# Attention steps of three, three and two key tiles in a two-layer graph network kernel

## The chip, the core and the metric

The kernel runs on one core of a Trainium2 chip. The core has a matrix engine (TensorE, "PE" in the profile; its weight loads are "PEld"), VectorE ("DVE"), ScalarE ("ACT"), GpSimd ("POOL") and SyncE ("SP", which here only issues DMAs). Each works through its own queue in order and waits for the others on semaphores. TensorE writes into PSUM, eight banks of 128 partitions by 512 fp32 numbers; VectorE and ScalarE read it from there. The metric is the device time of one execution in microseconds (us).

## The reference

Sixteen graphs of 1024 nodes with 256 features share one adjacency matrix. Layer 0 is an attention whose queries come through a graph product; layer 1 is a normalised graph convolution with two dense layers and two batch norms.

```python
# layer 0, on h = relu(layernorm(x)); fea = transpose(h)
c_adj = mean(fea, axis=1)
diff = c_adj[:, None, :] - c_adj[:, :, None]
A = abs(abs(sigmoid(diff) - 0.5) - 0.5) * 2.0
A_s = (A + transpose(A)) * 0.5
g = relu(einsum('bcn,bnm->bcm', fea, adj * A_s) * para)     # queries
k, v = split(h @ kv_w)                                      # 4 heads of 64
attn = softmax(q @ k^T * scale);  x = x + attn @ v
# layer 1, on h = relu(layernorm(x))
agg = einsum('nm,bmd->bnd', A_hat, h)                       # A_hat: normalised adj + eye
h1 = relu(batchnorm(agg @ W1.T + b1))
x = x + batchnorm(h1 @ W2.T + b2)
```

Everything is fp32.

## The kernel before

**Attention.** A unit is one graph, one pair of heads `k` (two heads of 64 rows) and one half `f` of the queries (512 columns): 16 x 2 x 2 = 64 units. The keys are eight tiles of 128. A step (`scores`, L1071) takes two key tiles: for each of them four 64x64 matmuls (two heads `e`, two halves `c` of the tile) write two PSUM banks (L1081), one per head, and one exponential of 128x1024 (L1089) turns both into a tile `p` in SBUF. The pool `ps_sc` holds two such score tiles, four banks; `ps_o` holds one bank for the output `o`, and `ps_mm` three for everything else: all eight. In the trace every matmul shows as two records (fp32 goes through the array twice), so a key tile has eight score records.

`Unit.add` (L1104) adds the `p` tiles into `acc` on VectorE, for the softmax's denominators. `Unit.values` (L1115) multiplies the `p` tiles of the step before with the values (L1124): a step on TensorE is scores of step s, then values of step s - 1, then background. At a unit's end `fold` sums `acc` on VectorE, `sums` sends two small matmuls (L1173) through TensorE, `finish`/`gather` and `add_output` put the result into `xs`.

**Order.** It is written out by hand: `attention` (L1240) runs over the steps and between them draws pieces of work from a generator, `background(b)` (L964), until their costs reach the amount `due` at this step. For graph `b` the background computes keys, values and queries of graph `b + 1` (`keys_values` L672, `queries` L537), layer 1's graph product and first dense layer of graph `b - 1` (`aggregate`, `hidden`), and the norm of graph `b + 2` (`summed` L943). The engines' queues get the instructions in exactly this order.

**Weights.** `weigh(b)` (L477) makes `adj * A_s` in eight blocks: per block two ScalarE `Abs` (L508), one `Tanh` (L516), one VectorE multiplication with an adjacency block (L495). `weave(main, (i, side))` draws one slot of `side` with each piece of `main` from the i-th on; `double` draws two slots at once.

**Squares.** `squares(b)` (L432) transposes the normed features in 32x32 squares on VectorE and writes them to DRAM through GpSimd's queue; `gathered` (L446) reads them back, transposed, as `ht`, through SP's queue. The buffers with the tag `para` (two of 128x512) hold the factor of the queries (`load_para`, multiplied in at L557) and temporaries of layer 1.

**A second version of both layers** (`shifted_attention`) follows under a branch that is taken only if the softmax without a shift overflowed; in these runs it isn't taken.

After attention, `second` computes the second dense layer and the output from about 2130 us on; the change doesn't touch it.

Of the kernel before, what the change touches and what calls it, by code (L numbers as in the profile page):

```python
# [10 lines left out]
F32 = mybir.dt.float32  # L11
# [6 lines left out]
P = 128  # L18
# [5 lines left out]
def gnn_two_layers_kernel(  # L24
# [74 lines left out]
    def layers(shifted):  # L99
# [14 lines left out]

        p4 = attn.enter_context(tc.tile_pool(name=f"p4_{kind}", bufs=4, side="right"))
        ps_sc = attn.enter_context(
            tc.tile_pool(name=f"ps_sc_{kind}", bufs=2, space=PSUM, side="right")
        )
# [83 lines left out]
        nc.sync.dma_start(out=kvw, in_=kv_w.rearrange("(k p) j -> p k j", p=P))  # L202
        rows = big.tile([P, NH, NT], F32, name="rows")

# [23 lines left out]

        deg_sm = big.tile([P, 6, NT], F32, name="deg")
        later = {}  # L230
        row, diag, col, deg, tmp_deg, dinv = (deg_sm[:, i, :] for i in range(6))

# [199 lines left out]
        def squares(b):  # L432

            for k in range(CC):
                sq = p1.tile([P, N], F32, tag="sq", name=f"sq_{b}_{k}")
                nc.vector.transpose(
                    sq.rearrange("p (i t s) -> p i t s", i=NS, s=SQ),
                    hs["a", b][:, :, k * P : (k + 1) * P].rearrange("p t (i s) -> p i t s", s=SQ),  # L440
                )
                nc.gpsimd.dma_start(out=hsq_d[b][:, k], in_=sq)
                for _ in range(3):
                    yield 0.0
# [32 lines left out]
        def weigh(b):  # L477
# [11 lines left out]
            for slot in range(2 * NH * NP + 1):  # L489
# [27 lines left out]
                yield 0.0  # L517

        AHEAD = 6
        IDLE = 28  # L520
# [443 lines left out]
        def background(b):  # L964

            if b == 0:
# [59 lines left out]
        def shifted_attention(b):  # L1026
            for hd in range(HEADS):
                k, e = divmod(hd, 2)
                r = slice(e * HD, (e + 1) * HD)
                for t in range(NT):  # L1030
                    name = f"{b}_{hd}_{t}"
                    sc = ps_sc.tile([P, N], F32, tag="sc", name=f"sc_{name}")
                    for g in range(NH):
                        nc.tensor.matmul(
                            sc[:, g * FB : (g + 1) * FB],
                            qs[b][k][r, t * P : (t + 1) * P],
                            ks[b][k][r, g * FB : (g + 1) * FB],
                            start=True,
                            stop=True,
                        )  # L1040
                    sm = p2.tile([P, 3], F32, tag="smx", name=f"smx_{name}")
                    nc.vector.tensor_reduce(sm[:, 0:1], sc, AX.X, ALU.max, negate=True)
                    pr = p4.tile([P, N], F32, tag="p", name=f"p_{name}")
                    nc.scalar.activation(
                        pr, sc, AF.Exp, bias=sm[:, 0:1], accum_out=sm[:, 1:2]
                    )
                    nc.vector.reciprocal(sm[:, 2:3], sm[:, 1:2])
                    pt = p4.tile([P, N], F32, tag="p", name=f"pt_{name}")
                    for g in range(NH):
# [21 lines left out]
        def scores(b, k, f, g):  # L1071


            made = []
            for m in (2 * g, 2 * g + 1):
                sc = ps_sc.tile([P, 2, FB], F32, tag="sc", name=f"sc_{b}_{k}_{f}_{m}")
                for e in range(2):
                    r = slice(e * HD, (e + 1) * HD)
                    for c in range(2):
                        part = slice(c * HW, (c + 1) * HW)  # L1080
                        nc.tensor.matmul(  # L1081
                            sc[part, e, :],
                            ks[b][k][r, m * P + c * HW : m * P + (c + 1) * HW],
# [3 lines left out]
                        )  # L1087
                pr = p4.tile([P, 2, FB], F32, tag="p", name=f"p_{b}_{k}_{f}_{m}")
                nc.scalar.activation(pr, sc, AF.Exp)  # L1089
                made.append(pr)  # L1090
            return made

        class Unit:
# [21 lines left out]
            def values(self, g, prs):  # L1115

                b, k, f = self.at
                if g == 0:
                    self.o = ps_o.tile([P, FB], F32, tag="o", name=f"o_{self.name}")
                for i, pr in enumerate(prs):  # L1120
                    m = 2 * g + i
                    for e in range(2):
# [7 lines left out]
                        )  # L1130
                if g == NG - 1:
                    self.os = p2.tile([P, FB], F32, tag="os", name=f"os_{self.name}")
# [107 lines left out]
        def attention():  # L1240

            units = [Unit(b, k, f) for b in range(B) for k in range(CC) for f in range(NH)]
            steps = [(u, g) for u in units for g in range(NG)]
            per_graph = CC * NH * NG
# [3 lines left out]
            for s in range(len(steps) + 2):  # L1248
                if s < len(steps):
# [10 lines left out]
                    made = scores(*unit.at, g)  # L1260
                    due = total * (s % per_graph + 1) / per_graph
                    if b == B - 1:
                        due -= 0.5 * min(s % per_graph + 1, (per_graph - 1 - s % per_graph) * 0.75)
                else:
# [13 lines left out]
                if before is not None:  # L1278
                    (last, g_last), prs = before
                    last.values(g_last, prs)  # L1280
                    if g_last == NG - 1:
# [431 lines left out]
```

## Time and profile before

| | |
|---|---|
| median of 3 runs | 2460.07 us (2460.07 to 2460.52) |
| profiled execution, timed | 2460.34 us |
| its span, first to last instruction | 2458.6 us |
| TensorE's clock granted | 0.993 of full speed |
| ScalarE waits for scores (L1089) | 649.5 us |
| VectorE busy | 2003.9 us |
| DMA, mean over the span | 178 GB/s |
| first and last score matmul | 54.1 and 2124.1 us |

In a timeline a row is a run of like instructions: start and length in us, engine, line, operation, tiles ("written<-read"), shapes, how many, and in brackets the idle time of the engine just before with what ended it. In the table of groups "x512 | 495.4, 1020 | 649.5 <-PE" reads: 512 instructions, 495.4 us busy, 1020 ns each on average, 649.5 us of idle time of that engine before them, ended by PE. Matmul records overlap, since the array is pipelined: a record of 0.59 us is followed by the next one after about 0.43.

### The profile page before, as it was taken

To read this page: it belongs to the slowest core of one execution; us is meant where nothing else is said; L and a number is where in the kernel's file an instruction comes from. 1 tells how busy PE (TensorE), PEld (TensorE's weight loads), DVE (VectorE), ACT (ScalarE), POOL (GpSimd) and SP (SyncE) were. 2 spreads that over 40 slices of the span, in tenths; PEclk is the share of its full clock that TensorE was granted. 3 is DMA by queue.
4 is the path that set the end of the run, shared out by engine and by line. 5 is a ranking of instruction groups with operands and counts; after the bars stand their busy time and mean duration, and the time that the engine had idled before them with its cause. 6 is when DMAs were issued, how large, how long until landed. Compare 5 with 4: busy or idle time off the path is not lost. (4 is left out here: it accounts for less than half of the span.)

```text
span 2458.6 us, 35932 instructions
## 1 busy us (share of the span) xinstructions
PE 2412.4 (98%) x13290; PEld 832.6 (34%) x13290; DVE 2003.9 (82%) x3103; ACT 1257.7 (51%) x1870; POOL 559.5 (23%) x645
## 2 busy tenths in 40 slices
PE   9999999999999999999999999999999999999994
PEld 4333333333333333333333333333333332334444
DVE  5678888988888888888898888888888878767775
ACT  7874554545464545445454546454454534335554
POOL 1381202111111212020211212121202103136652
PEclk9999999999999999999999999999999999999997
DMA  4675545363645554453536355544545353456559
GB/s 146 204 242 182 172 138 179 118 229 125 209 139 193 171 189 163 158 171 126 209 117 231 120 201 160 197 164 167 172 134 188 116 201 142 152 197 230 196 193 372
DMA packets 204553, 437.18 MB, mean 178 GB/s; under 512 B 21456, under 2 KB 96720, under 8 KB 200272
## 3 DMA queue, kind: packets, MB, share of 16 engines
q1 hardware_dynamic: 173328, 327.29, 39.7%
q0 software_dynamic: 31040, 107.50, 11.6%
q8 instruction: 107, 1.75, 0.3%
q14 instruction: 78, 0.64, 0.1%
HBM read 331.36 MB, written 103.35 MB: 177 GB/s over the span
## 5 line engine op out<-in xcount | busy, mean ns | idle before, releaser
L1089 ACT ACTIVATE p<-sc 128x1024 f32<-128x1024 f32 x512 | 495.4, 1020 | 649.5 <-PE sc L1081 649.5
L1113 DVE TENSOR_TENSOR acc<-acc,p 128x1024 f32<-128x1024 f32 x384 | 469.8, 1223 | 58.2 <-ACT p L1089 36.9
L1081 PE MATMUL sc<-q,k 64*64 64x512 f32 x4096 | 498.6, 602 | 0.5 <-ACT p L1089 0.5
L1124 PE MATMUL o<-p,v 128*64 128x512 f32 x2048 | 494.7, 604 | 0.0
L174 PE MATMUL pa<-aht,h_b 128*64 128x512 f32 x1536 | 346.0, 592 | 1.1 <-ACT h_b L368 1.1
L174 PE MATMUL pg<-w,x_h 128*64 128x512 f32 x1472 | 332.0, 592 | 0.0
L1081 PEld LDWEIGHTS sc<-q,k 64*64 64x64 f32 x4096 | 131.5, 132 | 336.4 <-issue 287.8
L1124 PEld LDWEIGHTS o<-p,v 128*64 128x64 f32 x2048 | 124.6, 136 | 297.7 <-issue 251.2
L1142 POOL DMA_DIRECT2D out_d<-os x58 | 32.9, 568 | 803.2 <-DVE os L1138 803.2
L495 DVE SCALAR_TENSOR_TENSOR w<-w,adj 128x1024 f32<-128x1024 f32 x128 | 164.9, 1288 | 46.1 <-ACT w L516 45.1
L174 PEld LDWEIGHTS pa<-aht,h_b 128*64 128x64 f32 x1536 | 110.1, 137 | 220.6 <-issue 207.8
L174 PEld LDWEIGHTS pg<-w,x_h 128*64 128x64 f32 x1472 | 105.7, 137 | 210.1 <-issue 198.4
L508 ACT ACTIVATE w<-cbc,csum 128x512 f32<-128x512 f32 x256 | 170.3, 716 | 0.0
L516 ACT ACTIVATE w<-w 128x1024 f32<-128x1024 f32 x128 | 135.6, 1059 | 2.5
L571 DVE TENSOR_TENSOR w<-w,w 128x1024 f32<-128x1024 f32 x112 | 134.6, 1232 | 1.5
L174 PE MATMUL pv<-kvw_f,ht 128*64 128x256 f32 x1024 | 116.1, 379 | 0.0
L174 PE MATMUL pk<-ht,kvw_f 128*64 128x512 f32 x512 | 115.2, 593 | 0.2 <-ACT ht L430 0.2
L174 PE MATMUL py<-at,w 128*64 128x512 f32 x464 | 112.6, 593 | 0.8 <-DVE at L729 0.7
L174 PE MATMUL py<-at,w1s 128*64 128x512 f32 x448 | 107.9, 595 | 0.0
L1453 ACT ACTIVATE yin_f<-yin_f,sm_f 128x512 f32<-128x512 f32 x128 | 93.5, 803 | 19.0 <-DMA yin_f<-y_d 17.0
L826 POOL DMA_DIRECT2D y_d<-y x112 | 61.6, 550 | 145.1 <-DVE y L846 75.8
L1160 DVE TENSOR_REDUCE part<-acc 128x16 f32<-128x512 f32 x128 | 87.8, 686 | 4.4
(197 smaller groups left out, 2968.6 us busy)
## 6 DMA issues: line engine op xcount, KB each, us to landing
aht<-aht_d SPq DMA_DIRECT2D x224, 512.0 KB
adj<-in_adj_dram SPq DMA_DIRECT2D x128, 512.0 KB
y_d<-y POOLq DMA_DIRECT2D x128, 256.0 KB, 3.0
yin_f<-y_d SPq DMA_DIRECT2D x32, 1024.0 KB
para<-in_para_dram SPq DMA_DIRECT2D x64, 256.0 KB
x_d<-x_x POOLq DMA_DIRECT2D x16, 1024.0 KB, 5.1
xo_f<-x_d SPq DMA_DIRECT2D x32, 512.0 KB
out_dram<-xo_f POOLq DMA_DIRECT2D x32, 512.0 KB, 11.1
```

The lines of the kernel that those rows point to most:

```text
L174: nc.tensor.matmul(dst[r], left[:, r], right, start=start, stop=stop)
L495: nc.vector.scalar_tensor_tensor(w, w, 1.0, a, op0=ALU.add, op1=ALU.mult)
L508: nc.scalar.activation(w[:, t, :].rearrange("p (t q) -> p t q", q=P), cbc[:, q * NT // NH : (q + 1) * NT // NH], AF.Abs, bias=csum[:, th * ...
L516: nc.scalar.activation(made[i], made[i], AF.Tanh, scale=-0.5 / C)
L571: nc.vector.tensor_sub(block(i)[part], block(x)[part], block(y)[part])
L826: nc.gpsimd.dma_start(out=y1_d[i][:, j, :], in_=y)
L1081: nc.tensor.matmul(sc[part, e, :], ks[b][k][r, m * P + c * HW : m * P + (c + 1) * HW], qs[b][k][r, f * FB : (f + 1) * FB], start=True, sto ...
L1089: nc.scalar.activation(pr, sc, AF.Exp)
L1113: nc.vector.tensor_add(self.acc, self.acc, pr)
L1124: nc.tensor.matmul(self.o[r, :], vs[b][k][:, m, r], pr[:, e, :], start=(m == 0), stop=(m == NT - 1),)
L1160: nc.vector.tensor_reduce(self.part[:, e, :], acc.rearrange("p (c s) -> p c s", s=SQ), AX.X, ALU.add)
L1453: nc.scalar.activation(y, y, AF.Relu, bias=sh[:, j : j + 1], scale=scale[:, j : j + 1])
```

## The change

A unit now has three steps, with key tiles (0,1,2), (3,4,5) and (6,7). A score tile is one PSUM bank, for one head, out of four; each has an exponential of its own (128x512). The `p` tiles get a pool of their own, `p6`, with five buffers (before: four). The schedule's amounts are restated by key tiles instead of steps. The small `sums` matmuls come at the end of a step instead of its middle.

`squares` works on half of the nodes at a time, in buffers of the tag `para` instead of one of their own, and its first half is woven into the norm. Row sums of the adjacency (`rows`, `deg`) move into a part of `stats1` that isn't yet in use. In the first graph the weights' first slots are drawn singly; in the others two slots are drawn ahead of the keys, and doubling starts one piece later. `shifted_attention` is adapted to the smaller score tiles.

```diff
+        p6 = attn.enter_context(tc.tile_pool(name=f"p6_{kind}", bufs=5, side="right"))
         ps_sc = attn.enter_context(
-            tc.tile_pool(name=f"ps_sc_{kind}", bufs=2, space=PSUM, side="right")
+            tc.tile_pool(name=f"ps_sc_{kind}", bufs=4, space=PSUM, side="right")
         )
...
-        rows = big.tile([P, NH, NT], F32, name="rows")
+        spare = stats1[:, HC - 1].rearrange("p a s -> p (a s)")[:, (B * NH - 10) * 6 :]
+        rows = spare[:, : NH * NT].rearrange("p (q t) -> p q t", t=NT)
...
-            for k in range(CC):
-                sq = p1.tile([P, N], F32, tag="sq", name=f"sq_{b}_{k}")
-                nc.vector.transpose(
-                    sq.rearrange("p (i t s) -> p i t s", i=NS, s=SQ),
-                    hs["a", b][:, :, k * P : (k + 1) * P].rearrange("p t (i s) -> p i t s", s=SQ),
-                )
-                nc.gpsimd.dma_start(out=hsq_d[b][:, k], in_=sq)
-                for _ in range(3):
+            HT = NT // 2
+            for half in range(2):
+                ts = slice(half * HT, (half + 1) * HT)
+                for k in range(CC):
+                    sq = p2.tile([P, FB], F32, tag="para", name=f"sq_{b}_{half}_{k}")
+                    sq = sq.rearrange("p (i t s) -> p i t s", i=NS, s=SQ)
+                    nc.vector.transpose(
+                        sq,
+                        hs["a", b][:, ts, k * P : (k + 1) * P].rearrange(
+                            "p t (i s) -> p i t s", s=SQ
+                        ),
+                    )
+                    nc.gpsimd.dma_start(
+                        out=hsq_d[b][:, k].rearrange("p (i t s) -> p i t s", i=NS, s=SQ)[:, :, ts],
+                        in_=sq,
+                    )
                     yield 0.0
...
+        GROUPS = (0, 1, 2), (3, 4, 5), (6, 7)
...
         def summed(b):
-            yield from Norm(b, True).all()
+            norm, turns = Norm(b, True).all(), squares(b)
+            yield from islice(norm, 6)
+            yield from weave(islice(turns, 2), (0, norm))
             differences(b)
             yield 0.0
-            yield from squares(b)
+            yield from turns
...
-            yield from weave(islice(products, 3), (0, islice(w, 1)))
+            yield from weave(islice(products, 3), (0, islice(w, 2)))
             gathered(b, 1)
-            yield from weave(islice(products, 3), (0, islice(w, AHEAD - 3)))
+            yield from weave(islice(products, 2), (0, islice(w, AHEAD - 4)))
...
-                yield from weave(islice(products, 4), (0, double(islice(w, 8))))
+                yield from islice(w, 2)
+                yield from weave(islice(products, 4), (0, islice(w, 4)))
...
+                yield from islice(w, 2)
                 yield from weave(islice(products, 4), (0, islice(w, 4)))
                 asked = queries(b + 1)
-                yield from weave(islice(asked, 7), (0, double(w)))
+                yield from weave(islice(asked, 7), (1, double(w)))
...
-            for m in (2 * g, 2 * g + 1):
-                sc = ps_sc.tile([P, 2, FB], F32, tag="sc", name=f"sc_{b}_{k}_{f}_{m}")
+            for m in GROUPS[g]:
+                pr = p6.tile([P, 2, FB], F32, tag="p", name=f"p_{b}_{k}_{f}_{m}")
                 for e in range(2):
+                    sc = ps_sc.tile([P, FB], F32, tag="sc", name=f"sc_{b}_{k}_{f}_{m}_{e}")
                     r = slice(e * HD, (e + 1) * HD)
                     for c in range(2):
                         part = slice(c * HW, (c + 1) * HW)
                         nc.tensor.matmul(
-                            sc[part, e, :],
+                            sc[part, :],
                             ks[b][k][r, m * P + c * HW : m * P + (c + 1) * HW],
                             qs[b][k][r, f * FB : (f + 1) * FB],
                             start=True,
                             stop=True,
                         )
-                pr = p4.tile([P, 2, FB], F32, tag="p", name=f"p_{b}_{k}_{f}_{m}")
-                nc.scalar.activation(pr, sc, AF.Exp)
+                    nc.scalar.activation(pr[:, e, :], sc, AF.Exp)
                 made.append(pr)
...
-                    due = total * (s % per_graph + 1) / per_graph
+                    whole = CC * NH * NT
+                    past = (NH * unit.at[1] + unit.at[2]) * NT + GROUPS[g][-1] + 1
+                    due = total * past / whole
...
-                            wait = 6 if opens else 4
-                            at_mid.setdefault(s + 3 + opens, []).append(last.sums)
+                            wait = 5 if opens else 4 if last.at[0] == 0 else 3
+                            at_end.setdefault(s + 2 + opens, []).append(last.sums)
```

More of the change, by code (lines that the diff above doesn't have):

```diff
@@ L227, in load_adj_t @@
             return tile_
-        deg_sm = big.tile([P, 6, NT], F32, name="deg")
+        dinv = big.tile([P, NT], F32, name="dinv")
         later = {}
-        row, diag, col, deg, tmp_deg, dinv = (deg_sm[:, i, :] for i in range(6))
+        row, diag, col, deg, tmp_deg = (
+            spare[:, (NH + i) * NT : (NH + i + 1) * NT] for i in range(5)
+        )
         def degrees():
@@ L432, in squares @@
         def squares(b):
-            for k in range(CC):
-                sq = p1.tile([P, N], F32, tag="sq", name=f"sq_{b}_{k}")
-                nc.vector.transpose(
-                    sq.rearrange("p (i t s) -> p i t s", i=NS, s=SQ),
-                    hs["a", b][:, :, k * P : (k + 1) * P].rearrange("p t (i s) -> p i t s", s=SQ),
-                )
-                nc.gpsimd.dma_start(out=hsq_d[b][:, k], in_=sq)
-                for _ in range(3):
+            HT = NT // 2
[13 more added lines that the diff above has]
+                        in_=sq,
+                    )
                     yield 0.0
@@ L1031, in shifted_attention @@
                     name = f"{b}_{hd}_{t}"
-                    sc = ps_sc.tile([P, N], F32, tag="sc", name=f"sc_{name}")
+                    scs = [
+                        ps_sc.tile([P, FB], F32, tag="sc", name=f"sc_{name}_{g}") for g in range(NH)
+                    ]
                     for g in range(NH):
                         nc.tensor.matmul(
-                            sc[:, g * FB : (g + 1) * FB],
+                            scs[g],
                             qs[b][k][r, t * P : (t + 1) * P],
@@ L1040, in shifted_attention @@
                         )
[L1041 to L1048, printed above, removed]
+                    sm = p2.tile([P, 6], F32, tag="smx", name=f"smx_{name}")
+                    for g in range(NH):
+                        nc.vector.tensor_reduce(sm[:, g : g + 1], scs[g], AX.X, ALU.max, negate=True)
+                    nc.vector.tensor_tensor(sm[:, 2:3], sm[:, 0:1], sm[:, 1:2], op=ALU.min)
+                    pr = p6.tile([P, N], F32, tag="p", name=f"p_{name}")
+                    for g in range(NH):
+                        nc.scalar.activation(
+                            pr[:, g * FB : (g + 1) * FB],
+                            scs[g],
+                            AF.Exp,
+                            bias=sm[:, 2:3],
+                            accum_out=sm[:, 3 + g : 4 + g],
+                        )
+                    nc.vector.tensor_add(sm[:, 5:6], sm[:, 3:4], sm[:, 4:5])
+                    nc.vector.reciprocal(sm[:, 2:3], sm[:, 5:6])
+                    pt = p6.tile([P, N], F32, tag="p", name=f"pt_{name}")
                     for g in range(NH):
@@ L1119, in values @@
                     self.o = ps_o.tile([P, FB], F32, tag="o", name=f"o_{self.name}")
-                for i, pr in enumerate(prs):
-                    m = 2 * g + i
+                for m, pr in zip(GROUPS[g], prs):
                     for e in range(2):
@@ L1130, in values @@
                         )
-                if g == NG - 1:
+                if g == len(GROUPS) - 1:
                     self.os = p2.tile([P, FB], F32, tag="os", name=f"os_{self.name}")
@@ L1242, in attention @@
             units = [Unit(b, k, f) for b in range(B) for k in range(CC) for f in range(NH)]
+            NG = len(GROUPS)
             steps = [(u, g) for u in units for g in range(NG)]
@@ L1260, in attention @@
                     made = scores(*unit.at, g)
-                    due = total * (s % per_graph + 1) / per_graph
+                    whole = CC * NH * NT
+                    past = (NH * unit.at[1] + unit.at[2]) * NT + GROUPS[g][-1] + 1
+                    due = total * past / whole
                     if b == B - 1:
-                        due -= 0.5 * min(s % per_graph + 1, (per_graph - 1 - s % per_graph) * 0.75)
+                        due -= 0.25 * min(past, (whole - past) * 0.75)
                 else:
```

## The prediction

> **What bounds the kernel now.** I read the page's busy table first, then its costliest groups, then the timeline of TensorE in one attention step, and last the two places where the scores meet ScalarE.
>
> ```profile
> PE 2412.4 (98%) x13290; PEld 832.6 (34%) x13290; DVE 2003.9 (82%) x3103; ACT 1257.7 (51%) x1870; POOL 559.5 (23%) x645
> ...
> L1089 ACT ACTIVATE p<-sc 128x1024 f32<-128x1024 f32 x512 | 495.4, 1020 | 649.5 <-PE sc L1081 649.5
> ...
> L1081 PE MATMUL sc<-q,k 64*64 64x512 f32 x4096 | 498.6, 602 | 0.5 <-ACT p L1089 0.5
> ```
>
> TensorE is the bound: it waits visibly for almost nothing, so what lengthens its queue lengthens the run. But 98% busy isn't 98% used. One step of graph 7, TensorE alone:
>
> ```profile
> 1010.02 1.95 PE L1081 MATMUL sc<-q,k 64*64 64x512 f32 x16
> 1011.90 1.94 PE L1124 MATMUL o<-p,v 128*64 128x512 f32 x8
> 1013.66 5.32 PE L174 MATMUL pg<-w,x_h 128*64 128x512 f32 x24
> 1018.91 1.09 PE L1081 MATMUL sc<-q,k 64*64 64x512 f32 x8
> ```
>
> The same stretch, weight loads of the undisturbed background product:
>
> ```profile
> 1013.67 0.14 PEld L174 LDWEIGHTS pg<-w,x_h 128*64 128x64 f32 x2 [0.29 <-issue]
> 1014.10 0.14 PEld L174 LDWEIGHTS pg<-w,x_h 128*64 128x64 f32 x2 [0.29 <-issue]
> 1014.52 0.14 PEld L174 LDWEIGHTS pg<-w,x_h 128*64 128x64 f32 x2 [0.29 <-issue]
> ...
> 1017.96 0.14 PEld L174 LDWEIGHTS pg<-w,x_h 128*64 128x64 f32 x2 [0.29 <-issue]
> ```
>
> From 1013.67 to 1017.96 there are ten intervals, so a pass of 512 columns takes 0.429 us. Records of scores start four at a time, those of values and products two at a time. The step holds 16/4 + 8/2 + 24/2 = 20 passes, 8.58 us, yet lasts 1018.91 - 1010.02 = 8.89. **0.31 us of a step is lost at changes of kind**: scores 1.88 - 4 x 0.429 = 0.16, values 1.76 - 1.72 = 0.05, product 5.25 - 5.15 = 0.10. The step from 1044.04 to 1051.22 holds only 16 passes, 6.86 us, and lasts 7.18: again 0.32, so this is a price per step, not per matmul.
>
> The other place is the start of attention, where two steps' scores stand back to back, first on TensorE and then on ScalarE:
>
> ```profile
> 54.09 1.95 PE L1081 MATMUL sc<-q,k 64*64 64x512 f32 x16
> 56.52 2.00 PE L1081 MATMUL sc<-q,k 64*64 64x512 f32 x16 [0.49 <-ACT p L1089]
> ...
> 55.47 1.92 ACT L1089 ACTIVATE p<-sc 128x1024 f32<-128x1024 f32 x2
> ```
>
> A third key tile finds all four score banks taken. It starts at 56.52, when the first exponential (55.47, 1.00 long) has ended at 56.47 and 0.05 has passed. Everywhere else two key tiles fit the banks, so this wait occurs once.
>
> **What the Trainium skill says.** "TensorEngine Tiling (Array Packing)", Tiling Modes: changing the tiling mode drains TensorE. The trace agrees: into and out of the 64x64 scores is where the 0.31 us goes. "TensorE: Matmul & The Clock Gate", Part 3: matmuls keep program order, only weight loads are pulled ahead. So a waiting score matmul holds everything behind it, as at 56.52. "ScalarE: Activation LUTs", What ACT_TABLE_LOAD costs: an activation with immediate operands takes 186 ns + 0.833 ns per element and neighbours overlap by 93; for 1024 that is 1039, against 1020 measured. "Trainium Kernel Development and Optimization", Performance Expectations: matmul busy time is a bad measure since matmuls are pipelined, which the 0.31 us inside a "busy" row shows.
>
> **The change, part by part.** Sums are against the profiled execution: span 2458.6 us, timed at 2460.34, 0.27 above the median of the runs, 2460.07.
>
> *Fewer steps.* 64 units had four steps each, 256; now three each, 192. TensorE's built order confirms it, with the same matmuls in all. 64 x 0.31 = **-20 us**. The row sums of the softmax (two small matmuls per unit) move from between scores and values to the step's end. They cost 0.14 us before (1036.90 to 1037.04) and I keep that; +-0.03 each would be +-2.
>
> *Three key tiles through four banks.* A step's scores now are six half tiles of one bank (one per head); four banks exist, as before. In the built order the fifth and the sixth matmul pair each wait for ScalarE: for the exponentials of the first and second half tile. Take the scores' start as 0.
> - Passes start at 0, 0.48 (the second after a fresh start takes 0.05 more: 1001.12 to 1001.61), 0.91, 1.34. The third tile would start at 1.77.
> - ScalarE starts on the first tile at 1011.17 - 1010.02 = 1.15; both heads finish together.
> - A half exponential isn't in the trace. Nearest rows: copies of 128x512 out of the same memory, 0.584 (L683), 0.569 and 0.588 (L574, L575), these two starting 0.46 apart (716.60, 717.06). I take 0.58 and 0.46. From below, 0.57 and 0.46; from above the skill's price, 0.61 and 0.52.
> - First half tile: 1.15 + 0.58 + 0.05 = 1.78 against 1.77, just in time. Second: 1.15 + 0.46 + 0.58 + 0.05 = 2.24, late by 0.47. After this fresh start its second pass again pays about 0.05: **0.53 us** (0.44 to 0.61).
>
> TensorE has nothing else to do there: values and background product stand behind in its queue. Two steps of each unit have three tiles: 128 x 0.53 = **+68 us** (56 to 78). Steps of two tiles don't wait.
>
> *What ScalarE has before it.* Any lateness of ScalarE was free with two tiles; with three it adds to the stall in full. Before, it is late where the weights are made doubly:
>
> ```profile
> 716.16 1.95 PE L1081 MATMUL sc<-q,k 64*64 64x512 f32 x16
> ...
> 717.54 1.34 ACT L508 ACTIVATE w<-cbc,csum 128x512 f32<-128x512 f32 x2
> 718.91 1.06 ACT L516 ACTIVATE w<-w 128x1024 f32<-128x1024 f32 x1
> 719.88 1.92 ACT L1089 ACTIVATE p<-sc 128x1024 f32<-128x1024 f32 x2
> ```
>
> Scores at 716.16, exponential at 719.88: 3.72 instead of 1.15. In graph 5 the sixteen steps are late by 0.7, 2.6 and 0.5 and by at most 0.1 elsewhere. The new order starts weights two slots earlier and doubles them later, so I walked it. Step 1 of a graph: six exponentials end near 4.0, then four 128x512 keys copies, three pairs of L508 and three L516; the last copy waits for a product done at about 12.0, one L516 follows, ending 14.1; the next scores start at 13.7. Step 2: query copies from 7.8, two pairs of L508 (1.34) and two L516 (1.06) end at 13.7, next scores at 12.9. ScalarE is free 0.4 and 0.8 after these starts, before 1.15. I take **0**; the bound is 3.8 us a graph over 15 graphs, 57.
>
> *Edits that I put at nothing.* The third exponential of a middle step reuses the fifth-last tile and waits until the values of the step before, queued behind the scores, have read it, some 1.4 us of ScalarE, 64 times; behind it stand ScalarE's background copies, needed only after the values, and ScalarE is 49% idle. Its 1024 half exponentials at 0.58 against 512 at 1.02 add 72 us of busy time to that idle time. Squares: 26 transposes of 1.24 become 52 of about 0.71 (L1138), +5 us on VectorE's 455 us of idle, and 26 more POOL issues of 0.59; the third half waits for the first half's write (about 3 us, as y's) with several VectorE operations between. Uncovered it would be 5 us, and a parameter load on SP could be late as much. Moving row-sum storage costs no instruction. The first graph's single weights take lateness of ScalarE off one step (exponential 4.6 us late there) that TensorE didn't wait in.
>
> Sum: 2460.3 - 20 + 68 = **2508**.
>
> **Rivals.** *A, the switches win (faster):* the second half tile's bank comes free in time. For: the first is on time within 0.01. Against: ScalarE must do two exponentials serially, 0.46 apart. It decides where the stall is under 20/128 = 0.16 us a step; with no stall, 2440. *B, ScalarE behind:* my walk has margins of 0.75 and 0.35 us; if the weights, keys or VectorE's takes slip past them, each slip is paid in full: half of the bound, +28, 2536; all, 2565. For: the 2.57 above; against: single slots now keep TensorE's pace. *C, no net change:* the edits don't have their effect or cancel; 2460.
>
> **How the numbers follow.** Main case 0.68, its own range 2494 to 2521 (stall 56 to 78, less 20, +-2 for the sums); A 0.12; B 0.18; C 0.02. The range 2488 to 2545 leaves out A and the far end of B. Within 0.2%, some 5 us, a measurement of this kernel can't be told from no change. Faster 0.12, same 0.02, slower 0.86.
>
> **What would show it.** Right: in TensorE's waits, scores waiting for p rise from 0.5 to tens of us in about 128 places (part of each is hidden inside pipelined records, so the sum shows less than 68); the timeline of a three-tile step shows its last score passes starting near 2.24; the loss per change stays 0.31. Wrong: those passes near 1.77 throughout (A); exponentials starting later than 1.2 after the scores in many three-tile steps (B); TensorE waiting for VectorE in the products.

## The result, and the profile after

| | before | after |
|---|---|---|
| median, us | 2460.21 (2460.07 to 2460.52) | 2535.0 (2533.43 to 2535.51) |
| ratio | | 1.0303 (95% interval 1.0285 to 1.0321) |
| span of the profiled execution, us | 2458.6 | 2531.3 |
| a graph in the middle (graphs 2 to 13), us | 134.4 | 137.7 |
| graph 0, graph 1, us | 105.5, 135.6 | 121.0, 140.8 |
| last transpose of the output to the end, us | 30.4 | 35.0 |

A graph's length is the time from its first score matmul to the next graph's, out of the trace's records; for graphs 2 to 13 it is the median. The change costs 75 us; 2508 was forecast, so 27 us are missing from the forecast's sum. Line numbers in what follows are those of the kernel that was run.

Busy times and groups of the kernel after (the second number after the bar is ns of one instruction, then the idle time before the group and what ended it):

```profile
PE 2466.2 (97%) x13290; PEld 866.9 (34%) x13290; DVE 2023.2 (80%) x3129; ACT 1295.4 (51%) x2382; POOL 589.8 (23%) x671
...
L1109 PE MATMUL sc<-q,k 64*64 64x512 f32 x4096 | 555.6, 606 | 12.4 <-ACT p L1116 12.3
L1116 ACT ACTIVATE p<-sc 128x512 f32<-128x512 f32 x1024 | 528.4, 606 | 587.1 <-PE sc L1109 505.4 <-PE o L1150 81.4
...
L1109 PEld LDWEIGHTS sc<-q,k 64*64 64x64 f32 x4096 | 148.8, 132 | 344.7 <-issue 177.6 <-ACT p L1116 145.3 <-ACT w L520 11.6
```

TensorE looks almost as busy as before, 97% against 98%, and its score matmuls (line 1109) seem to wait for ScalarE for 12.3 us only. The score rows have grown from 498.6 to 555.6 us with the same 4096 matmuls, and the third row shows where: the weight loads of the scores stood 145.3 us until ScalarE's exponentials (L1116). While head 0's matmul of a tile still runs, head 1's waits, and the row counts as busy. (The 145.3 us show the place, not the size: a weight load stands earlier than the matmul that needs it.)

A three-tile step of graph 5 in the timeline of the kernel after:

```profile
763.77 3.34 PE L1109 MATMUL sc<-q,k 64*64 64x512 f32 x24
...
764.89 3.04 ACT L1116 ACTIVATE p<-sc 128x512 f32<-128x512 f32 x6 [5.30 <-PE sc L1109]
765.54 0.19 PEld L1109 LDWEIGHTS sc<-q,k 64*64 64x64 f32 x4 [0.71 <-ACT p L1116]
766.03 0.20 PEld L1109 LDWEIGHTS sc<-q,k 64*64 64x64 f32 x4 [0.29 <-ACT p L1116]
767.03 1.94 PE L1150 MATMUL o<-p,v 128*64 128x512 f32 x8
```

The third key tile's head 0 loads its weights 1.77 us after the step's start, its head 1 at 2.26, both released by an exponential; the values follow at 3.26, where ScalarE began at 1.12. Six passes of 0.429 and the change of kind from scores to values of 0.16 would be 2.73: **0.53 us are lost**. Over all: 126 of the 128 three-tile steps stand alone; the first two of the run stand back to back and are left out. In 118 of them ScalarE starts 1.12 to 1.18 us after the scores ("on time"), and they lose 64.3 us, 0.545 each. In the other eight it starts at 1.5 to 7.1 us ("late"), and they lose 18.9: three in graph 0, two in graph 1, three in graph 14.

The worst of the eight, in graph 0:

```profile
109.80 1.21 DVE L507 SCALAR_TENSOR_TENSOR w<-w,adj 128x1024 f32<-128x1024 f32 x1
...
109.81 1.95 PE L1109 MATMUL sc<-q,k 64*64 64x512 f32 x16
...
111.03 0.34 SPq L228 DMA_DIRECT2D at<-in_adj_t_dram  x1
...
115.87 1.06 ACT L245 ACTIVATE at<-at 128x1024 f32<-128x1024 f32 x1 [4.96 <-DMA para<-in_para_dram]
...
116.92 2.04 ACT L1116 ACTIVATE p<-sc 128x512 f32<-128x512 f32 x4
117.55 2.46 PE L1109 MATMUL sc<-q,k 64*64 64x512 f32 x8 [5.79 <-ACT p L1116]
```

Scores at 109.81, the first exponential at 116.92. For 4.96 of these 7.11 us ScalarE stands in front of a column sum of the adjacency (L245, for the degrees), whose tile has not arrived. (The wait is put down to a parameter load; the sum reads the adjacency tile, whose load was issued just before that one.) SyncE's own waits between 95 and 125 us, before and after, say why the tile is late:

```profile
SPq L226 <- DVE w L495: 5.0, 1, 5.0
```

```profile
SPq L228 <- DVE w L507: 14.7, 2, 8.7
```

The adjacency tiles for the degrees and those for the weights share three buffers. In the new order SyncE waits up to 8.7 us (before: 5.0) until VectorE's multiplication for the weights (L507, done at 111.01) has freed one, and issues the load at 111.03. TensorE's matmuls for the fifth score bank then wait 5.79 us. Before, this step's exponential was on time (1.16 us after scores at 108.99); the latest one of graph 0 came 5.67 us after scores at 74.70, and with two tiles and two free score tiles it cost TensorE nothing.

TensorE's granted clock fell as well. Each row is a stretch with TensorE's busy time and instructions first and the granted clock third from the end:

```profile
115.63:122.45 6.82, 4.90 (x14) 1.35 (x16) 4.10 (x8) 4.18 (x8) 5.42 (x8) 0.50 1.01 389
153.18:156.59 3.41, 3.41 (x12) 1.20 (x10) 3.31 (x3) 0.95 (x2) 2.98 (x4) 0.50 0.75 260
```

```profile
119.94 3.17 PE L1150 MATMUL o<-p,v 128*64 128x512 f32 x8
122.94 3.60 PE L175 MATMUL pg<-w,x_h 128*64 128x512 f32 x16
```

The first stretch at half the clock begins in TensorE's longest wait in attention (5.79 us, until 117.55), the second 1.9 us after the end of the next longest (2.98, until 151.26). Eight values records at 119.94 take 3.00 us until the next matmul, instead of 1.76. If half of the 8.31 busy us is lost, the stretches cost an estimated 4.2 us, 1.2 of them inside the late step above. The kernel before has no such stretch ahead of 2385 us, and no such wait. In the traces of all fourteen kernels of this document it is the same: the six with TensorE waits of over 1.9 us in attention have such stretches there, the eight without have none. That the wait is the cause was not tested by itself.

### The profile page after: what moved, and what is told of

Read it like the earlier page. It is cut to its first block, busy times and chain, and to the rows that moved or that the text cites. A ratio compares the mean times of both kernels' runs of the same rounds, so it can differ in the third digit from the quotient of the medians.

```text
span 2531.3 us, 36595 instructions
## 1 busy us (share of the span) xinstructions
PE 2466.2 (97%) x13290; PEld 866.9 (34%) x13290; DVE 2023.2 (80%) x3129; ACT 1295.4 (51%) x2382; POOL 589.8 (23%) x671
## 5 line engine op out<-in xcount | busy, mean ns | idle before, releaser
L1116 ACT ACTIVATE p<-sc 128x512 f32<-128x512 f32 x1024 | 528.4, 606 | 587.1 <-PE sc L1109 505.4
L1109 PE MATMUL sc<-q,k 64*64 64x512 f32 x4096 | 555.6, 606 | 12.4 <-ACT p L1116 12.3
L1150 PE MATMUL o<-p,v 128*64 128x512 f32 x2048 | 484.5, 605 | 0.0
L1109 PEld LDWEIGHTS sc<-q,k 64*64 64x64 f32 x4096 | 148.8, 132 | 344.7 <-issue 177.6
L1150 PEld LDWEIGHTS o<-p,v 128*64 128x64 f32 x2048 | 130.4, 137 | 335.3 <-issue 312.6
L507 DVE SCALAR_TENSOR_TENSOR w<-w,adj 128x1024 f32<-128x1024 f32 x128 | 174.2, 1369 | 41.7 <-ACT w L528 40.5
L1137 DVE TENSOR_TENSOR acc<-p,p 128x1024 f32<-128x1024 f32 x64 | 78.4, 1225 | 85.1 <-ACT p L1116 85.1
L372 ACT ACTIVATE h_b<-x_x,lnsm_b 128x256 f32<-128x256 f32 x128 | 70.0, 603 | 80.1 <-DVE lnsm_b L361 80.0
L1482 ACT ACTIVATE yin_f<-yin_f,sm_f 128x512 f32<-128x512 f32 x128 | 93.5, 802 | 18.9 <-DMA yin_f<-y_d 16.3
```

The costliest lines, as they stand in the source:

```text
L507: nc.vector.scalar_tensor_tensor(w, w, 1.0, a, op0=ALU.add, op1=ALU.mult)
L1109: nc.tensor.matmul(sc[part, :], ks[b][k][r, m * P + c * HW : m * P + (c + 1) * HW], qs[b][k][r, f * FB : (f + 1) * FB], start=True, stop=True,
L1116: nc.scalar.activation(pr[:, e, :], sc, AF.Exp)
L1137: nc.vector.tensor_add(self.acc, self.held, pr)
L1150: nc.tensor.matmul(self.o[r, :], vs[b][k][:, m, r], pr[:, e, :], start=(m == 0), stop=(m == NT - 1),)
L1482: nc.scalar.activation(y, y, AF.Relu, bias=sh[:, j : j + 1], scale=scale[:, j : j + 1])
```

## The experiments

Each is compared with the kernel before in runs on the same chip (medians 2460.2 to 2460.5).

| | us | ratio to before |
|---|---|---|
| steps of two tiles, rest of the change | 2466.9 | 1.0028 (1.0018 to 1.0039) |
| one exponential for a whole key tile | 2536.2 (2529.1 to 2536.5) | 1.0299 (1.0281 to 1.0316) |
| short first exponentials | 2525.7 (one run) | |
| first exponential twice | 2620.3 (one run) | |
| values between the second and third key tile | 2503.5 (2499.9 to 2507.1) | 1.0172 (1.0155 to 1.0189) |
| column sums on VectorE | 2528.4 | 1.0277 (1.0261 to 1.0293) |
| two tiles in graphs 0 and 1 | 2515.9 | 1.0228 (1.0212 to 1.0243) |
| before, squares by halves | 2486.1 | 1.0105 (1.0090 to 1.0121) |
| before, the same woven in early | 2464.9 | 1.0019 (1.0012 to 1.0025) |
| before, row sums at the end | 2459.1 | 0.9995 (0.9987 to 1.0003) |
| before, row sums at the end, outputs by SyncE | 2457.4 | 0.9988 (0.9981 to 0.9995) |
| the same, 12 of 32 outputs by SyncE | 2462.2 (2458.7 to 2465.3) | 1.0007 (1.0000 to 1.0014) |

**The group size alone.** All of the change but the groups:

```diff
-        GROUPS = (0, 1, 2), (3, 4, 5), (6, 7)
+        GROUPS = (0, 1), (2, 3), (4, 5), (6, 7)
...
-                            wait = 5 if opens else 4 if last.at[0] == 0 else 3
+                            wait = 6 if opens else 4
```

> The changed kernel with steps of two key tiles again (four per unit); everything else of the change stays: half exponentials, squares, weights, sums at the step's end. Bank theory (the whole loss comes from the third key tile waiting for exponentials of the first): 2457 to 2461 us, within 0.2% of the kernel before, perhaps 3 us under it because the sums sit in TensorE's background. Rival (the loss comes from the other edits: half exponentials load ScalarE, squares and weights delay VectorE): stays above 2490.

2466.9: six to ten us over the expectation, but it splits the change. The groups are worth 2535.0 - 2466.9 = 68 of the 75 us. Of the other 6.7, graph 0 has 3.0 (the same column sum waits 4.5 us for its tile here) and the ending 5.2; the graphs in the middle last 134.30, 0.1 less than before. The late exponential is here too, 7.59 us after its scores at 109.06, but with two tiles that step loses nothing and the next one 0.6 us.

**What the third tile waits for.** Four edits of the kernel after. First, score tiles of two banks again, with one exponential of 1024:

```diff
-                    sc = ps_sc.tile([P, FB], F32, tag="sc", name=f"sc_{b}_{k}_{f}_{m}_{e}")
...
+                sc = ps_sc.tile([P, 2, FB], F32, tag="sc", name=f"sc_{b}_{k}_{f}_{m}")
...
-                    nc.scalar.activation(pr[:, e, :], sc, AF.Exp)
+                nc.scalar.activation(pr, sc, AF.Exp)
```

> The changed kernel with score tiles of two banks and one exponential of 1024 columns per key tile, two such tiles, steps of three, three and two. Bank theory: the third tile then waits for the first whole exponential, which starts 1.12 after the scores and takes 1.00, plus 0.05: 2.18 instead of 1.77, with 0.05 for the fresh start 0.46 per step against 0.53, so 128 x 0.07 = 9 us faster than the changed kernel, about 2526. Rival (half exponentials are what costs, through ScalarE's load): below 2500. Rival (halves are what limits the loss): above 2545.

A miss: the middle graphs are 137.57 instead of 137.68, and graph 0 lasts 4.6 us longer, where the profiled run has 17.1 us at half the clock instead of 10.2. (One of the four runs took 2529.1.) A whole exponential starts at 1.16 and takes 1.02, so both banks are free at 2.23; by halves the second is free at 2.26. Halves give the first bank back early but not the second, and the second decides. In this form TensorE's waits show what the halves hid (total, times, longest):

```profile
PE sc L1108 <- ACT p L1115: 53.5, 128, 6.1
```

128 places, as many as there are three-tile steps.

Second, less for ScalarE to do before the banks come free (half the columns of the first key tile then get the third one's probabilities):

```diff
-                    nc.scalar.activation(pr[:, e, :], sc, AF.Exp)
+                    short = m == GROUPS[g][0] and len(GROUPS[g]) == 3
+                    n = FB // 2 if short else FB
+                    nc.scalar.activation(pr[:, e, :n], sc[:, :n], AF.Exp)
+                    if m == GROUPS[g][-1] and len(GROUPS[g]) == 3:
+                        nc.scalar.activation(made[0][:, e, FB // 2 :], sc[:, FB // 2 :], AF.Exp)
```

> In steps of three tiles the first key tile's exponentials cover 256 columns alone; its other 256 columns are filled last, from the third tile's scores, so these probabilities are those of another key tile. ScalarE's work in columns is the same, two instructions more per such step. Bank theory: the second half tile's bank comes free at 1.12 + 0.26 + 0.37 + 0.05 = 1.80 against 1.77, a loss of about 0.08 instead of 0.53 per step: 128 x 0.45 = 57 us faster than the changed kernel, about 2478, or some less since ScalarE's lateness in the first graph stays. Rival (three-tile steps lose time elsewhere, in VectorE's additions or the buffers of p): 2525 or more.

In the step the mechanism is confirmed. Timeline:

```profile
766.28 2.91 PE L1109 MATMUL sc<-q,k 64*64 64x512 f32 x24
...
767.40 0.66 ACT L1118 ACTIVATE p<-sc 128x256 f32<-128x256 f32 x2 [3.24 <-PE sc L1109]
...
769.12 1.94 PE L1154 MATMUL o<-p,v 128*64 128x512 f32 x8
```

2.84 instead of 3.26; the 104 on-time steps lose 11.7 us in all, 0.11 each. But the total fell by 9 us only, in a single run, far less than expected. Much of the gain was given back in other places. ScalarE's six exponentials became eight with more busy time in all, and 22 steps were now late (34.1 us instead of 18.9); 23.9 us at half the clock, instead of 10.2, are in part inside these. And VectorE's additions, which need a tile's last exponential, came later, and so, by this reading, did what stands behind them in its queue:

```profile
PE py L175 <- DVE y L882: 13.8, 13, 1.1
PE py L175 <- DVE y L859: 6.6, 13, 0.8
```

The banks of layer 1's first dense layer (`py`) wait 20.4 us in all; in the kernel after it was 2.7, before nothing of this kind. Three-tile steps lose 37 us less than in the kernel after (83.1 to 45.8), `py` takes 18 of them back and the clock an estimated 6 at most (half of TensorE's busy time in these stretches, 10.1 against 4.2); some 6 us more are not assigned.

Third, more for ScalarE to do:

```diff
-                    nc.scalar.activation(pr[:, e, :], sc, AF.Exp)
+                    for _ in range(2 if e == 0 and m == GROUPS[g][0] and len(GROUPS[g]) == 3 else 1):
+                        nc.scalar.activation(pr[:, e, :], sc, AF.Exp)
```

> In steps of three tiles the very first half exponential is done twice. Bank theory: both waits of the third key tile move out by one spacing of 0.48, and TensorE with them: 128 x 0.48 = 61 us slower, about 2596. Rival (ScalarE's time isn't on the path there): under 2545.

+85 instead of +61, in the direction and place expected: middle graphs +5.04 us, 8 x 0.63. The size was off because the repeat starts 0.629 us after the first, not 0.48 as other neighbours do; it writes the same tile. On-time steps lose 1.171 us instead of 0.545, 0.626 more: what is added to the first tile's exponentials is paid by TensorE in full.

Last, work for TensorE in the place of the wait; `between` issues the values of the step before for its first key tile:

```diff
             for m in GROUPS[g]:
+                if len(made) == 2:
+                    between()
...
-                    last.values(g_last, prs)
+                    last.values(g_last, prs, early if s < len(steps) else 0)
```

> The changed kernel with the values of the step before split: those of its first key tile stand between the second and the third key tile's scores, so TensorE has 0.86 us of work and two changes of kind where it waits for score banks now. If the wait is for the first exponentials alone, the third tile's scores come at about 2.9 us after the step's start, past the 2.24 us at which the second bank is free: 126 stalls of 0.53 go (-67), some 0.5 us of each late exponential is hidden in the 8 late steps (-4), and 126 x 0.31 of changes of kind come back (+39): about 2503 us. If the stall comes from ScalarE being behind as such, it only moves on to the next wait and the changes of kind come on top: 2574 us.

2503.5 in the median, as expected, though the four runs lie 7 us apart. Timeline of a three-tile step:

```profile
757.96 1.95 PE L1111 MATMUL sc<-q,k 64*64 64x512 f32 x16
759.08 2.06 ACT L1118 ACTIVATE p<-sc 128x512 f32<-128x512 f32 x4 [5.30 <-PE sc L1111]
759.83 1.08 PE L1152 MATMUL o<-p,v 128*64 128x512 f32 x4
760.84 1.09 PE L1111 MATMUL sc<-q,k 64*64 64x512 f32 x8
761.86 1.08 PE L1152 MATMUL o<-p,v 128*64 128x512 f32 x4
```

Scores, values, scores, values without a wait. The inserted values take 1.01 us until the next scores and these 1.02 until the next values, where two passes are 0.858: 0.15 + 0.16 = 0.31 for the added round. Middle graphs fell to 135.81: 137.68 - 8 x 0.545 + 8 x 0.31 = 135.80. So both prices of the forecast, 0.53 for the stall and 0.31 for a round of kinds, are confirmed, and the stall is a wait for the first exponentials, not for ScalarE's throughput as such. The 4 us expected from the late steps did not come: graph 0 lasts 124.5 us in the profiled run, the slowest of the four, with 17.1 us at half the clock. It's still slower than before: a step that has to be split this way saves no change of kind.

**The late steps.** Column sums of the adjacency out of ScalarE's queue:

```diff
-                nc.scalar.activation(a, a, AF.Copy, accum_out=col[:, t : t + 1])
+                nc.vector.tensor_reduce(col[:, t : t + 1], a, AX.X, ALU.add)
```

> The changed kernel with the adjacency's column sums of the first graph made by VectorE (one reduction each) instead of ScalarE (one copy with accumulation each, 1.04 us). If ScalarE's queue is what makes the exponentials late in graphs 0 and 1, the step at 109.8 us (exponential 7.1 us after its scores) loses the two column sums that stand ahead of it, some 2 us, and the step at 146.3 us (4.3 us) loses about three, some 3 us: together about -5 us, 2530 us. If VectorE or a transfer holds those exponentials up, nothing is won, 2535 us, or a little is lost to VectorE's longer queue.

2528.4, -6.6. Graph 0 went from 121.0 to 115.4 us, the step at 109.8 is no longer late, and the eight late steps' 18.9 us are seven's 11.4. What was expected came out, for more than the reason given: with the two sums' work went ScalarE's wait for a tile, and one stretch of 3.4 us at half the clock is left of 10.2. Against that, TensorE now waits once, 2.8 us, for VectorE's row sums. Then, two-tile steps where most of the lateness is:

```diff
+        PAIRS = (0, 1), (2, 3), (4, 5), (6, 7)
+        def groups(b):
+            return PAIRS if b < 2 else GROUPS
...
-            for m in GROUPS[g]:
+            for m in groups(b)[g]:
...
```

> The changed kernel with steps of two key tiles in graphs 0 and 1 alone, three, three and two in the other fourteen. If the same lateness of ScalarE is harmless with two tiles and paid in full with three, graph 0 falls from 121.0 to about 108.5 us and graph 1 from 140.8 to about 135.5, what they last with two-tile steps everywhere: -18 us, 2517 us. If the excess of the first graphs came from the other edits (the weights drawn singly, the squares woven in), only the ordinary stall of sixteen steps goes, 16 x 0.53 less 8 x 0.31 of changes of kind: -6 us, 2529 us.

2515.9, with graph 0 at 108.8 and graph 1 at 135.5: the first case. Sixteen ordinary stalls less eight rounds of kinds are 16 x 0.53 - 8 x 0.31 = 6 us; the rest of the 19 is lateness of ScalarE that two-tile steps bear and three-tile steps don't, with the half clock that came with it (none in attention here). The exponential at 108.8 still comes 7.46 us after its scores.

**The squares and the ending.** On the kernel before, the squares by halves (the hunk of `squares` in the change, nothing else):

> The kernel before with one edit alone, the squares by halves of nodes through the factor buffers (52 transposes and 52 GpSimd-issued writes instead of 26 and 26). If the 4.6 us longer ending of the program (GpSimd's closing instructions, after the last output has landed) comes from the 26 more writes that GpSimd issues: 2464.8 us, +4.6, all of it after the last transfer. If the longer ending has another cause in the change: 2460.4 us, as before. If the halves delay the keys: more than 2465 us, with waits of TensorE for the transposed features.

2486.1: the last case by its size, with another cause. The ending is there: 35.2 us after the last transpose, instead of 30.4. And every middle graph is 1.6 us longer. VectorE's timeline in it:

```profile
1085.67 0.70 DVE L442 STREAM_TRANSPOSE sq<-x_h 128x512 f32<-128x512 f32 x1
...
1089.41 0.71 DVE L442 STREAM_TRANSPOSE sq<-x_h 128x512 f32<-128x512 f32 x1 [1.74 <-DMA hsq_d<-sq]
...
1093.82 0.68 DVE L754 TENSOR_TENSOR at<-pa,at 128x512 f32<-128x512 f32 x1
```

The third transpose stands 1.74 us until the first half's write has landed and its buffer is free; the operands of layer 1's first dense layer (L754) come late, and TensorE waits 18.0 us for them in 13 graphs. It isn't the keys that are late but what stands behind the transpose on VectorE. So the halves and the change's new place for the first half (the hunk of `summed`) together:

> The kernel before with squares by halves and, unlike the run with the halves alone (2486.1 us), with the change's place for the first half: woven into the norm. If the 1.6 us a graph that the halves alone cost come from VectorE standing at its third transpose until the first half's write has landed (1.74 us idle there), and the earlier place hides that wait: graphs back to 134.4 us, 2465 us, of which 4.6 us are the longer ending. If the waits only move: 2475 us or more.

2464.9, middle graphs 134.39. The groups of the two runs, without and with the new place:

```profile
L442 DVE STREAM_TRANSPOSE sq<-x_h 128x512 f32<-128x512 f32 x52 | 35.2, 696 | 22.7 <-DMA hsq_d<-sq 22.7
```

```profile
L442 DVE STREAM_TRANSPOSE sq<-x_h 128x512 f32<-128x512 f32 x52 | 34.8, 689 | 0.0
```

What is left, 4.7 us, is the ending. GpSimd's two long closing instructions have these lengths in the records:

| GpSimd issues | runs | semaphore, drain, us |
|---|---|---|
| 326 | after, and the runs with the halves | 1.61, 5.87, after the last output |
| 300 | before; row sums at the end | 0.71, 2.20, after the last output |
| 288 | 12 outputs by SyncE | 0.48, 1.22, after the last output |
| 268 | 32 outputs by SyncE | 1.57, 5.71, some 60 us before the end |

The last two rows have both of these edits of the kernel before, the row with 288 with `(nc.sync if b < 6 else nc.gpsimd)` in place of `nc.sync`; the run with the row sums at the end has the first alone:

```diff
-                            at_mid.setdefault(s + 3 + opens, []).append(last.sums)
+                            at_end.setdefault(s + 2 + opens, []).append(last.sums)
...
-                    nc.gpsimd.dma_start(
+                    nc.sync.dma_start(
                         out=by_rows(out[b], half), in_=xo
```

> The kernel before with one edit alone, the two small row-sum matmuls of a unit at the end of a step instead of between scores and values. In the traces a change of kind that they sit in costs 0.05 us less at the end of a step than in its middle (before: 0.110 into them, 0.052 between them, 0.031 to the values; after: 0.000, 0.001, and 0.132 instead of 0.100 to the scores), for 63 units: 3 us less, 2457 us. If the sums then come too late for what divides by them, no change or slower, 2460 us or more.

> The kernel before with the row sums at the end of a step (2459.1 us) and the 32 writes of the output issued by SyncE instead of GpSimd: GpSimd issues 268 transfers instead of 300 (the changed kernel: 326). Its closing instructions took 0.71 and 2.20 us at 300 and 1.61 and 5.87 us at 326. If they grow with the number of its transfers, they shrink further here, by up to 2.9 us (all that is left): 2456 us. If the number matters only past some point, they stay: 2459 us. SyncE then holds its later loads behind the writes, which could cost some us: 2465 us.

> As the run before, but only the first 12 of the 32 output writes are issued by SyncE: GpSimd issues 288 transfers. If its closing instructions grow with the number, about 0.18 us per transfer from the two points known (4.6 us for 26), they are 2.1 us shorter: 2457 us. If they depend on the last transfers alone, or on a point passed between 300 and 326, no change: 2459 us.

The row sums' place is worth 1.4 us, half of what was expected; the interval reaches 1, but the runs of the two kernels don't overlap. With SyncE issuing all outputs the time falls by some 1.5 us more (each against its own runs of before), to **2457.4, below the kernel before (0.9988) and the changed one**. The closing instructions don't get shorter by that; they move. GpSimd's drains in the run with the row sums at the end, and in this one (shortest, median and longest in ns, then first and last start):

```profile
L1709 POOLq DRAIN  x3: 40/107/2197, 2454.1 to 2456.9; - x3
```

```profile
L1709 POOLq DRAIN  x3: 40/107/5708, 2391.5 to 2455.8; - x3
```

The long one starts at 2391.5 us here, while outputs are still to come: GpSimd has nothing left to issue and closes early. From the end of the last transfer to the end of the span it is 2.9 us now, instead of 4.5. It takes nearly as long as in the kernel after, with 58 issues fewer, so the number of issues alone doesn't set the length. With 288 it is 1.2 us shorter after 12 issues fewer (2.1 was expected), but the output phase got longer and uneven, and nothing is won. What sets the length isn't shown.

## Why the prediction was right in direction and 27 us short

On the spans the change costs 72.7 us; the forecast had 47.7.

| step of the forecast | forecast, us | measured, us | from |
|---|---|---|---|
| fewer rounds of kinds, 64 x 0.31 | -20 | -20 | scores of two tiles last 1.878 as before; the split values confirm 0.31 |
| third key tile waits, 128 x 0.53 | +68 | +68.5 | 0.545 in 118 steps (64.3), and the eight late ones' own share, 8 x 0.53 |
| ScalarE's lateness | 0 | +14.6 | 18.9 less that share; 1.2 of it is the half clock |
| TensorE at half the clock, the rest | not named | +3 | estimate, 4.2 less those 1.2 |
| squares, the ending | 0 | +4.6 | the closing instructions |
| row sums moved | 0 | -1.4 | that edit alone |
| VectorE late for `py` | 0 | +2.7 | TensorE's waits, 13 x 0.2 |
| not assigned | | +1 | |

**The term that failed is ScalarE's lateness, taken as 0.** The walk behind it went through one graph of the middle, and for these it holds: in all three-tile steps of graphs 2 to 13 ScalarE starts by 1.18 us, and these graphs are 3.28 us longer, where 8 x 0.53 - 4 x 0.31 makes 3.0. But it was summed over all sixteen as if they had the same order. Graphs 0 and 1 hold the degrees besides, graph 14 has a background of its own. There the exponentials start up to 7.1 us after the scores, and each us past the usual 1.1 is paid, as the rival B said; B was right in its mechanism and wrong in its place (the weights of every graph). That its 2536 meets the result is half chance: lateness brought 15, not 28.

The forecast had said that making the first graph's weights singly takes lateness of ScalarE off one step. That came true: the exponential that was 4.6 us late at 74.70 has no counterpart now (the step at 81.98 starts its own after 1.12). But another step, on time before, is late by 6.0 us. The trace says by what: a multiplication for the weights on VectorE stands before the release of an adjacency buffer, and a load, a column sum and six exponentials behind it. The late step is there in the run with two tiles and not in those with the squares' edits or the row sums' place alone; the order of the weights was not undone by itself, so its part in this is read, not shown.

**A term that is not in the forecast is TensorE's clock**, at half for 10.2 us of graph 0, about the waits there. It goes with the lateness: the runs without long waits don't have it.

**The squares at nothing** was right inside the graphs and named the right danger, the third half behind the first half's write. Without the cover it costs 2486.1 - 2464.9 = 21 us, not the 5 that the forecast gave. What wasn't seen is that GpSimd's closing instructions get 4.6 us longer with the halves, after the last transfer, where nothing covers them.

The other edit put at nothing held in size: ScalarE's wait for a free `p` tile was to be 64 x 1.4 = 90 us, and its row above shows 81.4 until the values (L1150). The low end of the stall's range, 0.44, is 0.46 by the figures it names; nothing hangs on that.

**The sign in the profile:** forecast were scores waiting "in about 128 places" for tens of us. TensorE's waits of the kernel after show 12.3 us in 8, since the wait lies between the two heads' matmuls, inside a busy row. It's to be found in the weight loads (145.3 us) and measured by the distance between scores and values.

Rival A (no stall) fell with the 118 steps at 0.545: the first bank came back in time, the second 0.48 later. Rival C fell with the result.

## What to carry to other kernels

Before giving a step more tiles than there are banks, work out when the *last* bank that it reuses comes free: two exponentials in series on one engine give the second one back later by the distance of their starts (0.48 us here), and that wait outweighs a saved change of kind, here 0.53 against 0.31 / 2 per three-tile step. Slack in buffers also carries all irregular lateness of the engine behind them; list each late consumer in the trace before, over all stages and not one typical graph, and charge it in full once the slack is gone. And where a busy row grows with the same number of instructions, look at the weight loads: a wait between parts of one run of matmuls doesn't show as idle time. What an engine does to close can be taken off the end if its last work comes early enough: here 7.3 us of it moved 60 us forward.

## What the runs showed of the hardware that was not expected

- An exponential of 128x512 took 0.606 us on average, where the forecast took 0.58 from copies; a step's first two started 0.493 apart, the next ones 0.477. The Trainium skill ("ScalarE: Activation LUTs", What ACT_TABLE_LOAD costs) gives an estimate of 186 + 0.833 x 512 = 612 ns, and 519 apart with its overlap of 93; the length agrees, the distance is shorter in the trace. The same exponential done twice into the same columns started 0.629 apart: no overlap at all.
- A change of kind around small matmuls: row sums between scores and values cost 0.110, 0.052 and 0.031 us at their three borders; between background and scores 0.000, 0.001 and 0.132, where scores straight after background cost 0.100. A part of the gain is taken back: the values' second pass starts 0.480 us after the first when scores stand before it, 0.459 after row sums.
- GpSimd's closing instructions took 7.3, 1.7, 2.9 and 7.5 us at 268, 288, 300 and 326 issued transfers. At 268 they stood some 60 us before the end, ahead of the last outputs' transfers.
- TensorE's granted clock was 0.50 in stretches of 6.83 and 3.41 us that began in a wait of 5.79 us and 1.9 us after one of 2.98.
